# Four tiles in the first head's convolution, two of its three results stored from SyncE, and the first keys loaded over three queues

## The chip, the cores and the metric

The kernel runs on one core of a Trainium2 chip. The metric is the device time of one launch in microseconds (us). Engines are named as in the profile: PE is TensorE, DVE is VectorE, ACT is ScalarE, POOL is GpSimd, SP is SyncE. DMAs can be issued from SP, ACT and POOL; the profile calls their queues q1 (SP), q10 (ACT) and q0 (POOL).

## The reference

The input `x` has 48 channels of 256 x 256 pixels in float32. Two layers follow each other, each added to its input. Only the first touches the change:

```python
qkv = einsum('bchw,oc->bohw', group_norm(x), w_qkv)       # 48 -> 144 channels
qkv = depthwise_conv3x3(qkv, w_dw)
q, k, v = (heads(t) for t in split(qkv, 3))   # 4x4 patches, pad 4: 8 heads of 96 rows x 4356 patches
q, k = q / |q|, k / |k|
attn = softmax(einsum('bhcn,bhcm->bhnm', q, k) * temperature)
out = fold(einsum('bhcn,bhnm->bhcm', v, attn))
x = x + einsum('bchw,oc->bohw', out, w_proj)
```

The second layer normalises again and mixes 64 x 64 windows over width, height and channel. The 260 patches that lie wholly in the padding are zero, so the kernel works on the other 4096 only.

## The kernel before, in words

The program runs in stages. First it loads `x`, takes the group statistics, and writes the pointwise convolution of the first two heads to a tensor in DRAM (`t1`). Then `depthwise_first` (L358) does the depthwise convolution of head 0. Then the attention runs head by head, with the convolution of the next head woven into it by a hand-written order. The output projection and the second layer close the program.

`depthwise_first` works on ten "rows" (`Depthwise(0, r, dg)`). A row is 126 partitions (7 bands of the image x 18 channels: 6 each of q, k and v) of 4 x 256 pixels, and the bands lie 36 image lines apart. For each row the steps are:

- `load` (L209, issued from SP) brings 6 lines with margins into a tile `pad`.
- The nine taps are done either on VectorE (even rows: `first` on ACT, L215, then eight `tap`, L234) or as 18 matmuls with diagonal matrices on TensorE (odd rows, L223).
- `square` (ACT, L245), `reduce` (DVE, L249), `norm` (a matmul, L253) and `root` (L257 to L262) give the factor `y`.
- `scale` (DVE, L279) writes `o`, re-ordered to 16 x 64 per partition.
- `high` (ACT, L288) rounds `o` to `oh`; `low` (here on POOL, L292) writes the remainder `ol`.
- `store` (L297) issues three DMAs of 504 KB, of `oh`, `ol` and `o`, to the DRAM tensor `qkv[0]`. Each partition's 16 x 64 values go out as 16 pieces of 256 bytes, 2560 bytes apart.

The tiles come from the pool `dg`. The class takes their number from one line: `self.bufs` is 2 with a pool, and `pad` has twice as many (4). A tile can be written again when its last reader, a store included, is done. The order of the instructions on each engine in this stage is fixed when the program is built, by a scheduler that looks at the dependencies; the queues then run in that order.

After this stage every engine reads the value `large` and branches past a code path for large temperatures that isn't taken (L465). Then the attention's prologue loads the first query block (six DMAs on SP), the eight key tiles of head 0 and two value tiles:

```python
load_query(0, 0)
for m in range(NM):
    load_key(0, m, nc.scalar if m % 2 else nc.sync)
for m in range(2):
    load_value(0, m)
    turn(0, m)
```

`load_key(h, m)` issues four or eight DMAs (L313), eight where its 512 columns cross a border between two bands in `qkv`: four for tiles 0 and 7, eight for the others, 56 in all. They read what the stores wrote, so all wait for the landed stores. `scores` (L339) then multiplies queries and keys, `weigh` (L570) the exponentials and values.

Of the kernel before, what the change touches and what calls it, by code (L numbers as in the profile page):

```python
# [43 lines left out]
def conv_preact_kernel(  # L44
# [15 lines left out]
    nc = tc.nc  # L60
# [103 lines left out]
    def both_halves(t, y, n, base=0):  # L164

        return [t[:, base + s * HALF + y : base + s * HALF + y + n, :] for s in range(2)]

    class Strip:


        def __init__(self, j):
            self.j = j
# [20 lines left out]
        def store(self):  # L193
            for s, rows in enumerate(both_halves(t1[1], 2 * self.j, 2, base=1)):
                nc.sync.dma_start(out=rows, in_=self.ot[:, 2 * s : 2 * s + 2, :])

    class Depthwise:


        def __init__(self, h, r, pool=None):  # L200
            self.h, self.r = h, r
            self.pool, self.bufs = (pool, 2) if pool else (cv, 1)

        def load(self):
            g = [i for i, (h0, h1) in enumerate(GROUPS) if h0 <= self.h < h1][0]
# [85 lines left out]
            self.ol = self.pool.tile([NP1, KK, PX], F32R, name="ol", tag="t4", bufs=self.bufs)  # L291
            eng.tensor_sub(self.ol, self.o, self.oh.bitcast(F32))  # L292

        def store(self, parts=(0, 1, 2)):
            px = slice(self.r * PX, (self.r + 1) * PX)
            for i in parts:
                nc.gpsimd.dma_start(  # L297
                    out=qkv[self.h][i].rearrange("j (c k) n -> (j c) k n", k=KK)[:, :, px],
                    in_=self.o if i == 2 else (self.ol if i else self.oh).bitcast(F32),
                )  # L300
# [16 lines left out]
    def load_keys(kt, h, m, eng=nc.sync):  # L317
        col = m * 512, (m + 1) * 512
        k0, k1 = (qkv[h][i, :, HD : 2 * HD] for i in range(2))
        to = kt.bitcast(F32)  # L320
        load(to[0:HD, 0, :], k0, *col, eng)
        load(to[HD:128, 0, :], k1[:, 0:32], *col, eng)
        load(to[0:64, 1, :], k1[:, 32:], *col, eng)
        load(to[64:128, 1, :], k1[:, 32:], *col, eng)
# [35 lines left out]
    def depthwise_first():  # L360

        with tc.tile_pool(name="dg", bufs=1) as dg, tc.tile_pool(name="dps", bufs=3, space=PSUM) as dps:
            diag = dg.tile([NP1, 9, NP1], F32, name="diag")
            for t in range(9):
                nc.gpsimd.tensor_scalar_mul(diag[:, t, :], ident[:NP1, :NP1], dwt[:, 0, t : t + 1])
            rows = [Depthwise(0, r, dg) for r in range(CR + 1)]
            for d in rows[:2]:
                d.load()
            for i in range(0, CR + 1, 2):
                a, b = rows[i : i + 2]  # L370
                b.taps_on_tensor(diag, dps.tile([NP1, 2, 512], F32, name="dps"))
                a.first()
                for t in range(1, 9):
                    a.tap(t)
                for d in rows[i + 2 : i + 4]:
                    d.load()
                for d in (a, b):
                    d.square()
                    d.reduce()
                    d.norm()  # L380
                    d.root(on_scalar=True)
                    d.scale()
                    d.high()
                    d.low(nc.gpsimd)
                    d.store()


    with tc.tile_pool(name="xn", bufs=1) as xnp, tc.tile_pool(name="cst", bufs=1) as cst, tc.tile_pool(
# [10 lines left out]
        for j in range(0, HALF, LR):  # L399
            for s in range(2):  # L400
                eng = nc.sync if s == 0 else nc.scalar
# [10 lines left out]
        for g, (w, k) in enumerate(((wq, P2), (wr, C))):  # L412
            m = w.shape[1]
# [42 lines left out]
    cv = attention.enter_context(tc.tile_pool(name="cv", bufs=1))  # L456
# [3 lines left out]
    for t in ots:  # L460
        nc.gpsimd.memset(t[:, :, 0:1], 0.0)
        nc.gpsimd.memset(t[:, :, W + 1 : W + 2], 0.0)
    depthwise_first()

    with tc.If(nc.values_load(large) > 0):  # L465
# [33 lines left out]
    with tc.tile_pool(name="ahead", bufs=2) as ah, tc.tile_pool(name="ae", bufs=3) as ae, tc.tile_pool(  # L499
# [7 lines left out]
        def load_key(h, m, eng=nc.sync):  # L507
            keys[h, m] = ah.tile([128, 2, 512], F32R, name="kt", bufs=14)
            load_keys(keys[h, m], h, m, eng)
# [81 lines left out]

        load_query(0, 0)
        for m in range(NM):
            load_key(0, m, nc.scalar if m % 2 else nc.sync)
        for m in range(2):
            load_value(0, m)
            turn(0, m)
# [9 lines left out]
        with tc.manual_schedule():  # L607
            load_query(0, 1)
            block = scores(0, 0)
            for h in range(NH):  # L610
                more = h + 1 < NH
                rows = {r: Depthwise(h + 1, r) for r in range(CR + 1)} if more else {}
                for g in range(NG):
                    p, d, n = rows.get(g - 2), rows.get(g - 1), rows.get(g)
# [42 lines left out]
                    for k in range(NK):  # L657
# [25 lines left out]
                        if g == 0 and h > 0 and k == 0:  # L683
                            for m in range(6, 8):
                                store(h - 1, m)
                        if g == NG - 1 and k > 0:
                            for m in range(2 * k - 2, 2 * k):
                                store(h, m)
            for m in range(6, 8):
                store(NH - 1, m)  # L690
# [69 lines left out]
    with tc.tile_pool(name="lx", bufs=2) as lx, tc.tile_pool(name="lz", bufs=2) as lz, tc.tile_pool(  # L760
# [14 lines left out]
        xqs, rts, zts, blks, parts = {}, {}, {}, {}, {}  # L775
# [150 lines left out]
```

## Time and profile before

| | us |
|---|---|
| median of 3 runs (3830.28 to 3836.73) | 3835.93 |
| the profiled execution | 3845.87 |
| its span | 3844.1 |
| first store of `depthwise_first` issued | 188.0 |
| last one issued | 288.6 |
| first key load issued (ACT) | 301.4 |
| PE busy in the span | 3525.9 (92%) |
| DVE busy | 2199.1 (57%) |
| ACT busy | 1717.9 (45%) |
| POOL busy | 583.3 (15%) |

The 40 slices of the page show TensorE at nine tenths or more from the sixth slice (480 us) to the thirty-fourth; the first four slices hold the statistics, the pointwise convolution and `depthwise_first`. A share over the whole span says little on the change, which lies between 145 and 330 us: that stage is to be read by itself.

### The profile page before, as it was taken

The numbers are of one execution on the slowest core, as the hardware profiler recorded it, in microseconds if no ns is written. First come the engines' busy times: TensorE is split into PE (matmuls) and PEld (weight loads), VectorE is DVE, ScalarE is ACT, GpSimd is POOL, SyncE is SP. The second block draws the span as 40 slices with busy tenths as digits, with TensorE's granted clock in tenths as the row PEclk, the third lists the DMA queues.
The fourth block names the chain that finished last, engine by engine and source line by source line (L and its number), as shares of the span: only waits on it lengthen the run. The fifth ranks groups of instructions, "written<-read, shape, count | busy, mean of one in ns | idle before, by whom it ended". The sixth has DMA issues, their size and how long they took to land.

```text
span 3844.1 us, 99863 instructions
## 1 busy us (share of the span) xinstructions
PE 3525.9 (92%) x44216; PEld 2927.6 (76%) x44216; DVE 2199.1 (57%) x3520; ACT 1717.9 (45%) x2668; POOL 583.3 (15%) x535
## 2 busy tenths in 40 slices
PE   1856999999999999999999999999999999755998
PEld 0324777788888888888888888888888888514776
DVE  5562776169727962994399359826972222365553
ACT  0223565555545544554455455545554444200222
POOL 0150212012201220221022112201220000000111
PEclk9877999999999999999999999999999999866999
DMA  6475676534523443444244325433542000598555
GB/s 142 153 163 144 178 196 179 175 109 117 119 81 101 119 110 87 104 120 98 83 117 115 94 81 128 111 88 92 128 113 75 24 18 22 116 238 141 111 105 100
DMA packets 280235, 441.66 MB, mean 115 GB/s; under 512 B 57354, under 2 KB 205082, under 8 KB 276336
## 3 DMA queue, kind: packets, MB, share of 16 engines
q1 hardware_dynamic: 225150, 260.52, 26.7%
q0 software_dynamic: 48896, 165.90, 19.2%
q10 hardware_dynamic: 5746, 8.73, 1.0%
q8 instruction: 351, 5.75, 0.6%
q14 instruction: 92, 0.75, 0.1%
HBM read 234.76 MB, written 199.95 MB: 113 GB/s over the span
## 4 chain that ended last, share of the span: by engine, by line
PE 73%; issue 10%; DMA 8%; DVE 2%; SPq 1%; POOL 0%; ACT 0%; POOLq 0%; ACTq 0%; DVEq 0%
PE big L339 32%; PE big L570 31%; DMA lxq<-x1s 3%; PE pb L826 3%; PE pa L804 2%; PE big L183 2%; DMA pot<-os__70 2%; PE pc L843 1%; DMA qkv<-o 1%; DMA pxt<-in_x_dram 1%; PE pst L524 1%; PE pt L587 1%; PE pn L253 1%; DMA xs<-in_x_dram 1%; DMA kt<-qkv 1%
## 5 line engine op out<-in xcount | busy, mean ns | idle before, releaser
L541 ACT ACTIVATE e<-big,nmx 128x1024 f32<-128x1024 f32 x1024 | 1144.0, 1117 | 846.2 <-PE big L339 636.4
L339 PE MATMUL big<-kt,qt 128*128 128x512 f32 x6144 | 1441.9, 394 | 57.9 <-DMA kt<-qkv 54.9
L570 PEld LDWEIGHTS big<-vn,e 128*64 128x64 f32 x32768 | 1364.8, 137 | 87.7 <-ACT e L541 45.1
L570 PE MATMUL big<-vn,e 128*64 128x96 f32 x32768 | 1422.7, 248 | 9.1 <-ACT ot L186 4.0
L339 PEld LDWEIGHTS big<-kt,qt 128*128 128x128 f32 x6144 | 1147.9, 189 | 322.0 <-issue 63.1
L581 DVE TENSOR_TENSOR oacc<-big,oacc 128x768 f32<-128x768 f32 x480 | 458.2, 955 | 708.7 <-PE big L570 708.7
L234 DVE SCALAR_TENSOR_TENSOR acc<-pad,dwt,acc 126x1024 f32<-126x1024 f32 x600 | 779.3, 1300 | 34.2 <-ACT acc L215 18.5
L292 POOL TENSOR_TENSOR ol<-o,oh 126x1024 fp32r<-126x1024 f32 x80 | 189.9, 2373 | 909.1 <-DVE ss L249 810.1
L554 DVE TENSOR_REDUCE zt<-zs 128x1 f32<-128x4 f32 x256 | 38.8, 152 | 368.5 <-ACT e L541 368.5
L811 DVE TENSOR_TENSOR lzt<-pa,cbias 128x864 f32<-128x864 f32 (+1 forms) x88 | 136.3, 1621 | 134.5 <-PE pa L804 134.5
L541 ACT ACTIVATION_READ_ACCUMULATOR e<-big,nmx 128x1 f32 x1024 | 196.3, 192 | 0.0
L833 ACT COPY lyt<-pb 128x512 f32<-128x512 f32 x144 | 84.3, 586 | 250.0 <-PE pb L826 250.0
L297 POOL DMA_DIRECT2D qkv<-o x80 | 101.0, 1262 | 567.8 <-DVE zu L556 348.7
L245 ACT ACTIVATE sq<-acc 126x1024 f32<-126x1024 f32 x75 | 79.3, 1058 | 171.7 <-issue 111.6
L279 DVE TENSOR_TENSOR o<-acc,y 126x1024 f32<-126x1024 f32 x75 | 149.4, 1992 | 11.0 <-DMA qkv<-o 11.0
L826 PEld LDWEIGHTS pb<-wsb,lzt 128*64 128x64 f32 x2304 | 132.1, 143 | 28.1 <-issue 21.1
L715 PE MATMUL pps<-pot,wp 96*96 96x512 f32 x128 | 77.9, 778 | 77.6 <-DMA pot<-os__70 77.6
L826 PE MATMUL pb<-wsb,lzt 128*64 128x128 f32 x2304 | 147.9, 287 | 1.3 <-issue 1.3
L186 ACT ACTIVATE ot<-big,bias 108x1024 f32<-108x1024 f32 x64 | 71.0, 1112 | 147.8 <-PE big L183 68.2
L804 PE MATMUL pa<-csn,lxq 48*128 48x144 f32 x1024 | 95.1, 333 | 33.9 <-DMA lxq<-x1s 32.6
L590 POOL DMA_DIRECT2D os__70<-oo x64 | 32.6, 514 | 615.4 <-ACT oo L589 615.4
L715 PEld LDWEIGHTS pps<-pot,wp 96*96 96x96 f32 x128 | 26.9, 218 | 128.0 <-issue 126.4
(115 smaller groups left out, 1897.6 us busy)
## 6 DMA issues: line engine op xcount, KB each, us to landing
pad<-t SPq DMA_DIRECT2D x80, 761.9 KB
qkv<-o POOLq DMA_DIRECT2D x80, 504.0 KB, 6.9
qkv<-oh POOLq DMA_DIRECT2D x80, 504.0 KB, 7.4
qkv<-ol POOLq DMA_DIRECT2D x80, 504.0 KB, 9.1
t<-ot SPq DMA_DIRECT2D x128, 217.7 KB
qt<-qkv SPq DMA_DIRECT2D x176, 96.0 KB
xs<-in_x_dram SPq DMA_DIRECT2D x128, 96.0 KB
os__70<-oo POOLq DMA_DIRECT2D x64, 192.0 KB, 2.8
```

Of the source, the lines that this page charges most:

```text
L234: nc.vector.scalar_tensor_tensor(self.acc, self.pad[:, dy : dy + KS, dx : dx + W], dwt[:, self.h, tap : tap + 1], self.acc, ALU.mult, ALU.add,
L279: nc.vector.tensor_tensor(self.o.rearrange("p (a b) x -> p a b x", a=KS), self.acc.rearrange("p a (x b) -> p a b x", b=KS), self.y.rearran ...
L292: eng.tensor_sub(self.ol, self.o, self.oh.bitcast(F32))
L297: nc.gpsimd.dma_start(out=qkv[self.h][i].rearrange("j (c k) n -> (j c) k n", k=KK)[:, :, px], in_=self.o if i == 2 else (self.ol if i else ...
L339: nc.tensor.matmul(ps[:, i, :], lhsT=qt[:, r, q0 : q0 + 128], rhs=kts[2 * j + i][:, r // 2, :], start=(r == 0), stop=(r == 2),)
L541: nc.scalar.activation(e[:, j * 1024 : (j + 1) * 1024], ps.rearrange("p a b -> p (a b)"), AF.Exp, bias=nmx[:, b : b + 1], accum_out=zs[:, ...
L570: nc.tensor.matmul(ps[p : p + 64, j // 4, j % 4 * HD : (j % 4 + 1) * HD], lhsT=e[:, mb * 128 + p : mb * 128 + p + 64], rhs=vn, start=(i == 0),
L581: nc.vector.tensor_add(oaccs[h, k], ps[:, :, : 4 * HD], oaccs[h, k])
L715: nc.tensor.matmul(ps[:, i : i + 2, :], lhsT=wp, rhs=ot[:, ki * KS + i : ki * KS + i + 2, :], start=True, stop=True,)
L804: nc.tensor.matmul(pa[:, s, i * T3 * C : (i + 1) * T3 * C], lhsT=xq[r, y0 + i, :], rhs=csn[r], start=True, stop=True,)
L811: nc.vector.tensor_tensor(zv[:, :, y0 : y0 + n, :], pa[:, :, : n * T3 * C].rearrange("p s (y k) -> p s y k", y=n), cbias.rearrange("p (u v ...
L826: nc.tensor.matmul(pb[s * WS : (s + 1) * WS, i, :], lhsT=zts[u][:, t * C + c + i, :], rhs=wsb[:, t, :], start=True, stop=True,)
```

## The change

It has three parts. The convolution of head 0 gets four tiles of each kind instead of two (and eight `pad` instead of four). Its stores are issued one by one: `oh` from SP right after `high`, `ol` from POOL as before, `o` from SP. The first key tiles go round over ACT, SP and POOL (tiles 0, 3, 6; 1, 4, 7; 2, 5), 20, 20 and 16 DMAs.

```diff
-            self.pool, self.bufs = (pool, 2) if pool else (cv, 1)
+            self.pool, self.bufs = (pool, 4) if pool else (cv, 1)
...
-        def store(self, parts=(0, 1, 2)):
+        def store(self, parts=(0, 1, 2), eng=nc.gpsimd):
             px = slice(self.r * PX, (self.r + 1) * PX)
             for i in parts:
-                nc.gpsimd.dma_start(
+                eng.dma_start(
...
                     d.high()
+                    d.store((0,), nc.sync)
                     d.low(nc.gpsimd)
-                    d.store()
+                    d.store((1,))
+                    d.store((2,), nc.sync)
...
         for m in range(NM):
-            load_key(0, m, nc.scalar if m % 2 else nc.sync)
+            load_key(0, m, (nc.scalar, nc.sync, nc.gpsimd)[m % 3])
```

In the built program SP issues the ten `pad` loads first and then the twenty stores, in the order `o`, `oh`, `oh`, `o` for each pair of rows; POOL issues the ten `ol` stores, each after its subtraction. On VectorE the scalings of rows 3, 5 and 7 stand ahead of taps and reductions that they followed before. The other heads' convolutions take their tiles from another pool, and their stores and key loads are as they were.

## The prediction

> **What bounds the kernel now.** I read the chain that ended last first, then the stage table, then engine and DMA lines. From 332 us on the chain is TensorE at work (busy 455.7 of 468 us between 332 and 800), and the change leaves that loop alone. Before it lies a hole: the chain passes from store to store of `depthwise_first`, then from key load to key load.
>
> ```profile
> 251.14 9.91 DMA qkv<-o
> ...
> 268.06 13.49 DMA qkv<-o
> ...
> 288.60 12.52 DMA qkv<-o
> ...
> 327.72 2.05 PE big L339 x4
> ```
>
> Columns: start, length, what. The last store lands at 301.1, the last key feeds TensorE at 327.7. Whatever moves 327.7 moves the end by as much. First what holds the stores, on VectorE (start, length, instruction, idle before and its releaser), then per stage:
>
> ```profile
> 261.14 1.22 DVE L279 TENSOR_TENSOR o<-dps,y 126x1024 f32<-126x1024 f32 x1 [0.66 <-DMA qkv<-o]
> ...
> 274.42 1.97 DVE L279 TENSOR_TENSOR o<-acc,y 126x1024 f32<-126x1024 f32 x1 [11.05 <-DMA qkv<-o]
> 281.67 1.23 DVE L279 TENSOR_TENSOR o<-dps,y 126x1024 f32<-126x1024 f32 x1 [5.28 <-DMA qkv<-o]
> ```
>
> ```profile
> 255.00:301.00 46.00, 2.73 (x9) 1.30 (x7) 8.33 (x11) 7.30 (x9) 24.07 (x16) 0.55 0.77 155
> 188.00:255.00 67.00, 57.80 (x136) 25.43 (x135) 62.77 (x56) 16.58 (x21) 37.08 (x24) 0.92 0.70 172
> ```
>
> The last three scalings wait 17.0 us for an `o` tile whose store hasn't landed: two tiles are too few. Before 255 VectorE is busy 62.8 of 67 us, so it is the limit there. But the DMA share (last but one column) is 0.77 after 255: the stores are nearly a limit themselves. So I priced them by queue, 188 to 301 us:
>
> ```profile
> q0 software_dynamic: 4800, 15.52, 65.2%
> q1 hardware_dynamic: 519, 3.03, 7.3%
> ```
>
> 65.2% of 113 us x 16 engines is 1179 engine-us for 30 stores: 2.46 us of all 16 each. A store is 2016 runs of 256 B, 126 an engine: 19.5 ns a run, and a packet (160 per store) holds 12.6 runs.
>
> **What the Trainium skill says.** (1) "DMA: Bandwidth & Descriptors", the section on why a DMA increments its semaphore by 16: a DMA from SP or ACT uses the largest k up to 16 that divides the slowest dimensions of both sides. The pads (source outermost 7) agree, in the window 156 to 160:
>
> ```profile
> DMA packets 127, 0.74 MB, mean 186 GB/s; under 512 B 7, under 2 KB 7, under 8 KB 127
> ```
>
> Seven small closing packets per load, and a share of 0.444, about 7/16. For a store from SP, with 126 and 2016, k is 14; no run of before shows it. (2) Same page, "Queues, rings and completion order": queues take turns on an engine packet by packet; one ring is consumed in order. So stores on SP stand behind pads on SP. (3) Same page, "Why small descriptors are slow (HBM only)": each packet costs about 3 cycles beside 8 for 256 B. In the trace hardware packets hold one run, software packets 12.6, so the moved stores lose that sharing. (4) Same page, "Issuing engines are not separate DMA queues": spreading saves issue time only. Here issue is what the first keys lack (below).
>
> **The change, part by part.**
>
> *Four tiles.* Pads go from 4 to 8; `sq`, `ss`, `o`, `oh`, `ol` from 2 to 4; instruction counts stay. Removed: the 17.0 us of waits. VectorE's own work runs out at 263.4; without the waits the last `o` comes one dependent chain later, about 265 (y of row 9 near 263.4, scale 1.2), `oh` 1.04 later at 266, `ol` 2.33 later at 268, its issue 1.35. The scheduled order also takes `o` of rows 3, 5 and 7 ahead of taps, 5 to 10 us earlier. What is late next is the DMA. Pads: 4.2 us each on 7 engines (780 KB at 186 GB/s). Eight go out at once; rows 8 and 9 wait for the first two pads (free by 172), so these 7 engines carry pads until 150 + 10 x 4.2 + 3 = 195.
>
> *Stores from SP.* 20 of 30 leave GpSimd (20 issues of 1.23 to 1.48 us: 27 us off POOL, which is not on the path except for the last 2.7). On SP they are queued behind all ten pad issues, and nothing else of SP's waits there. Price of a 256 B run in a packet of its own, from loads, as before has no such store: low end
>
> ```profile
> q10 hardware_dynamic: 90, 0.02, 9.5%
> ```
>
> (302 to 303 us: 1.52 engine-us / 90 = 17 ns), and a mixed window, 2340 to 2345,
>
> ```profile
> q1 hardware_dynamic: 687, 0.27, 24.6%
> ```
>
> 19.7 engine-us / 687 = 28.6 ns at a mean of 393 B; at the pads' 186 / 7 = 26.6 GB/s an engine the 137 B in excess take 5 ns off. I take 24 ns, with ends 17 and 40 (twice the software run: a write may cost more than a read). A store is then 144 runs x 24 = 3.5 us of engines 0 to 13. A row costs these 2 x 3.5 + 2.46 (`ol`, still GpSimd) = 9.4 us. Ten rows from 195: 195 + 94 + 2 to land = 291, against 301.1: **-10 us**. Rows arrive in time for it (row 4 is scaled at 230, four rows are served by 233), so the DMA is the bound, no more VectorE. At 17 ns a row is 7.4, the arrivals decide, and it is about 281; at 40 ns it is 14, and 337.
>
> *SP arrives later at the branch.* Now SP is free at 222.8 and pays for the skipped branch under cover:
>
> ```profile
> L465 SPq EVENT_SEMAPHORE  x8: 17/17/17, 229.8 to 234.9; - x8
> L465 SPq TENSOR_LOAD <-large x1: 899/899/899, 222.8 to 222.8; - x1
> ```
>
> From the load of `large` to ready is 12 us. After the change it begins at SP's last store issue. In the later stage SP issues two loads of 1536 runs in 1.5 us and is then held, 3.7 us per load, so only some 200 runs an engine are taken in advance: SP is held until about 284, ready at 296, 5 us after the landing. **+5 us** on the queries; the keys on ACT and GpSimd don't wait for it. If the DMA is fast, this is hidden (266 + 12 = 278).
>
> *Keys on three queues.* 56 loads, 28 each on SP and ACT, at 0.74 and 0.82 us an issue:
>
> ```profile
> 301.41 22.85 ACTq L313 DMA_DIRECT2D kt<-qkv  x28
> ...
> 304.48 20.70 SPq L313 DMA_DIRECT2D kt<-qkv  x28
> ```
>
> SP and ACT share eight completion semaphores in the compiled program, each DMA waiting for the one eight before; GpSimd has eight of its own. Hardware issues fall from 62 (with six of queries) to 46: 16 fewer at 24 us / 62 = 0.39 is **-6 us**. GpSimd's 16 cost 0.52 each, 8 us, and land in 3.5 (from its later key loads); it has nothing else to do. From SP's start: queries 3, 20 keys at 0.55 = 11, landing 3, a last pair of logits 1: 18 us. So 296 + 18 = 314, against 327.7: -14; without SP's delay the DMA (4.6 MB at 200 to 250 GB/s, 20 us) gives 291 + 21, much the same.
>
> *Sum*: -10 + 5 - 6 is -11, and 20 SP issues at 0.55 instead of 0.74 with fewer ahead of them make the other 3: -14. The profiled execution is 3845.9 (span 3844.1) and becomes 3832; the median shown is 3835.9, so 3822. The loop after 332 starts earlier by this and its own waits (pads at 342.9, strips at 468) are relative to its start.
>
> **The rivals.**
>
> *The stores aren't a limit* (17 to 20 ns, landing near 281): for it the 17 ns window; against it that these were loads, 90 of them, beside little else. SP ready at 288, keys by 306: -22 us, 3814. Chance 0.25.
>
> *My sum* (21 to 27 ns): -8 to -20 us, 3822. Chance 0.37.
>
> *Gains cancel* (27 to 31 ns, or SP held longer): landing 298 to 308, change within 7.7 us, 3836. Chance 0.15.
>
> *Slower: hardware stores of 256 B runs become the bound.* At 40 ns a store is 5.8, a row 14, landing 337, keys 337 + 21 = 358: +30 us, 3866. It decides from 327.7 - 21.5 = 306, that is (306 - 197) / 10 = 10.9 a row, 4.2 a store, 29 ns a run. For it: 1536-run loads of 512 B in the last stage took 58 ns a packet (3500 to 3540 us: 117.6% of 640 engine-us / 12928); against it both windows above. Chance 0.23.
>
> That four tiles change nothing (the DMA alone set the pace) is part of the third: the last three rows would merely wait elsewhere.
>
> **How the numbers follow.** 0.2% is 7.7 us, about what a measurement of this kernel can tell from no change. Faster: the first two, 0.61 of 0.62. Same: 0.15, with 0.01 more. Slower: 0.23. The predicted time is the second case, 3822; its own range is 3816 to 3828. The range reaches down to the best case less a few us of keys, 3804, and up to 35 ns a run, landing 318 and +14, with a few us for SP, 3852.
>
> **What would show it.** Right: no VectorE wait for `qkv<-o`; last `o` near 265; queue q1 with about 2016 + 14 packets per moved store, 22 to 27 ns each; the last landing an SP store near 291; first key logits on ACT's loads, SP's queries up to 5 us after the landing; last key wait near 313. Wrong: q1 above 30 ns a packet, or a last landing past 306; then the stores should have stayed. If `ol` on GpSimd lands last, the ring and turn argument is wrong.

## The result and the profile after

The changed kernel takes 3819.33 us (median of 10 runs, 3815.44 to 3830.9) against 3835.18 us for the kernel before (10 runs, 3829.95 to 3844.42): 0.996 of the time, 95% interval 0.9947 to 0.9974, or about 16 us less. The profiled executions are 3816.70 (span 3814.9) and 3845.87 us. Their difference of 29 us is more than the medians differ by; 6 to 7 us of it arise in the last stages of the program, which the change doesn't touch. So the reading below stays in the stage between the first pad and the first logits.

VectorE's last scalings first (start, length, instruction; an idle time in brackets would follow). They answer to the 11.05 and 5.28 us of waits shown of before:

```profile
262.02 1.97 DVE L279 TENSOR_TENSOR o<-acc,y 126x1024 f32<-126x1024 f32 x1
264.89 1.23 DVE L279 TENSOR_TENSOR o<-dps,y 126x1024 f32<-126x1024 f32 x1
```

No wait for a store is left, and the last `o` is scaled at 264.89 instead of 281.67. Now SP's own timeline in the same form:

```profile
186.81 18.98 SPq L297 DMA_DIRECT2D qkv<-oh  x2
...
271.05 6.56 SPq L297 DMA_DIRECT2D qkv<-o  x1
286.05 3.02 SPq L313 DMA_DIRECT2D qt<-qkv  x6
289.12 16.89 SPq L313 DMA_DIRECT2D kt<-qkv  x20
```

SP's last store is issued at 277.6. Between there and the queries lies the skipped branch, by the trace's instructions of line 467 (the former 465):

```profile
L467 SPq EVENT_SEMAPHORE  x8: 17/17/17, 284.1 to 285.4; - x8
L467 SPq TENSOR_LOAD <-large x1: 1199/1199/1199, 277.7 to 277.7; - x1
```

The chain that ended last (start, length, what) goes from the queries and keys to the last wait of TensorE, which was at 327.72 before:

```profile
286.91 3.22 DMA qt<-qkv
...
305.24 3.15 DMA kt<-qkv
...
308.42 2.17 PE big L339 x7
```

Before and after don't begin this stage at the same moment: the first pad is issued at 149.52 before and at 147.82 after, and the stages ahead of it scatter by some us from run to run. From here on times are therefore counted from the first pad issue. **Ready** is the first key load on ACT (all stores landed, all engines past the branch), **stage** is the last wait of TensorE for a key, and **keys** is the difference. Each comes from one profiled execution.

| | last `o` scaled | ready | keys | stage |
|---|---|---|---|---|
| before | 132.2 | 151.9 | 26.3 | 178.2 |
| after | 117.1 | 137.7 | 22.9 | 160.6 |

The stage is 17.6 us shorter: 14.2 to ready, 3.4 with the keys.

### The profile page after: what moved, and what is told of

Its sections match the earlier page's. It is cut to its first block, busy times and chain, and to the rows that moved or that the text cites. A ratio compares the mean times of both kernels' runs of the same rounds, so it can differ in the third digit from the quotient of the medians.

```text
span 3814.9 us, 99860 instructions
## 1 busy us (share of the span) xinstructions
PE 3522.9 (92%) x44216; PEld 2924.4 (77%) x44216; DVE 2201.3 (58%) x3520; ACT 1717.0 (45%) x2668; POOL 566.6 (15%) x531
## 4 chain that ended last, share of the span: by engine, by line
PE 72%; issue 11%; DMA 8%; SPq 1%; DVE 1%; ACT 0%; POOL 0%; ACTq 0%; POOLq 0%
PE big L339 32%; PE big L572 31%; PE pb L828 3%; DMA lxq<-x1s 3%; PE pa L806 2%; DMA t<-ot 1%; PE big L183 1%; DMA pot<-os__70 1%; PE pc L845 1%; DMA pxt<-in_x_dram 1%; PE pst L526 1%; PE pt L589 1%; PE pn L253 1%; DMA x1s<-pxt 1%; SPq L313 0%
## 5 line engine op out<-in xcount | busy, mean ns | idle before, releaser
L297 POOL DMA_DIRECT2D qkv<-o x70 | 86.0, 1229 | 508.8 <-DVE zu L558 236.3
L828 PEld LDWEIGHTS pb<-wsb,lzt 128*64 128x64 f32 x2304 | 132.3, 143 | 28.6 <-issue 21.5
```

The lines of the kernel that those rows point to most:

```text
L297: eng.dma_start(out=qkv[self.h][i].rearrange("j (c k) n -> (j c) k n", k=KK)[:, :, px], in_=self.o if i == 2 else (self.ol if i else self. ...
L828: nc.tensor.matmul(pb[s * WS : (s + 1) * WS, i, :], lhsT=zts[u][:, t * C + c + i, :], rhs=wsb[:, t, :], start=True, stop=True,)
```

## The experiments

Three questions were put. Which of the three parts brought the gain: do the tiles and SP need each other, as the prediction's sum has it, or does one of them do it alone? Is the software queue what the stores lost their time to? And does SP, with its stores behind the pads, bound the new kernel? Each expectation says what its letters stand for in its own run. Two programs were profiled twice; their ready and stage differ by up to 1.5 us, so less than 2 us is not read.

### Each part alone

Only the four tiles (`e1_tiles`):

```diff
-            self.pool, self.bufs = (pool, 2) if pool else (cv, 1)
+            self.pool, self.bufs = (pool, 4) if pool else (cv, 1)
```

> Only the four tiles; all thirty stores on GpSimd, keys on two queues. Measure: from the first pad issue of the first head to the last key load that TensorE waits for (178.2 us before, 160.6 us with the whole change). Theory A (the waits for a free tile held the stage, and GpSimd's stores keep up): no VectorE wait for a store, last scaling about 117 us after the first pad, last GpSimd issue 10 us later, landing 12 us after it, keys 26 us: about 165, that is -13 us in the stage and in the time. Rival B (the DMA rate held it, tiles only move the waits): about 176, -2 us or less.

Only `oh` and `o` on SP, with two tiles and the keys on two queues (`e2_sp`):

```diff
                     d.high()
+                    d.store((0,), nc.sync)
                     d.low(nc.gpsimd)
-                    d.store()
+                    d.store((1,))
+                    d.store((2,), nc.sync)
```

> Only the move of two stores to SP; two tiles, keys on two queues. Theory A: the waits for a free tile stay, and a tile now waits for stores that share 14 engines in ring order, so VectorE's waits grow from 17 us; the stage is 178 to 186 us long, time 0 to +8 us. Rival B (the gain of the whole change is the faster issue from SP): 165 to 170, -8 to -13 us.

Only the keys (`e3_keys`):

```diff
-            load_key(0, m, nc.scalar if m % 2 else nc.sync)
+            load_key(0, m, (nc.scalar, nc.sync, nc.gpsimd)[m % 3])
```

> Only the first keys over three queues. Theory A (the eight completion semaphores that SP and ACT share set the pace of the key loads): last store landed to last key falls from 26.6 to about 21 us, time -5 us. Rival B (the keys move at the rate of the DMA engines, or are held by SP's queries): 25 to 26.6 us, time -1 us or none.

Tiles and SP, with the keys as before (`e4_nokeys`, the changed kernel with the last line taken back):

> The whole change without its last part: four tiles, two stores on SP, keys on two queues. Theory A: 3 to 5 us longer than the whole change in the stage (164 to 166), time -12 us against before. Rival B (the third queue does nothing, since SP comes late to the branch and its queries decide): 161, time as with the whole change, -16 us.

| | last `o` scaled | ready | keys | stage | time, ratio to before (95%) |
|---|---|---|---|---|---|
| `e1_tiles` | 120.7 | 148.6 | 25.3 | 173.9 | 0.9986 (0.9975 to 0.9997) |
| `e2_sp` | 121.0 | 139.1 | 26.9 | 166.0 | 0.9954 (0.9935 to 0.9972) |
| `e3_keys` | 132.3 | 152.7 | 24.1 | 176.8 | 0.9982 (0.9973 to 0.9992) |
| `e4_nokeys` | 118.8 | 139.8 | 26.1 | 165.9 | 0.9952 (0.9934 to 0.9969) |

The move of two stores to SP is worth 12.2 us in the stage by itself. The four tiles are worth 4.3 alone and nothing on top of SP (165.9 against 166.0), though two tiles had been named as what holds VectorE. How that can be is in the profiles. With the tiles alone VectorE's last scalings come without a wait:

```profile
264.01 1.97 DVE L279 TENSOR_TENSOR o<-acc,y 126x1024 f32<-126x1024 f32 x1
266.87 1.23 DVE L279 TENSOR_TENSOR o<-dps,y 126x1024 f32<-126x1024 f32 x1
```

Against before they are 11.4 us earlier (counted from the first pad), but the stores don't land earlier by as much. Two windows of `e1_tiles` (start to end, length, then PE, PEld, DVE, ACT, POOL busy and in brackets the instructions, the TensorE clock, the share of the 16 DMA engines, GB/s), POOL's last store, and ACT's first key:

```profile
255.00:280.00 25.00, 6.23 (x17) 2.94 (x15) 6.95 (x10) 5.80 (x8) 20.01 (x14) 0.65 0.93 177
280.00:295.00 15.00, 0.00 (x0) 0.00 (x0) 0.00 (x0) 0.00 (x0) 0.00 (x0) 0.50 0.59 124
```

```profile
277.36 1.88 POOL L297 DMA_DIRECT2D qkv<-o  x1
```

```profile
294.72 22.10 ACTq L313 DMA_DIRECT2D kt<-qkv  x28
```

The software queue runs at a share of 0.93 and is still 15 us behind when POOL has issued its last store, so it isn't POOL's issuing that holds the stores. The share is 0.59 over these 15 us; the DMA view doesn't tell the engines apart, so whether some of them had run dry is not shown. From the last scaling to ready it takes 27.9 us, 8 more than the 19.7 of before. So the waits of VectorE were a sign of late landings, and the additional tiles only moved the queue from in front of VectorE to behind it.

With SP and only two tiles the landings are early enough for two tiles nearly to do. One wait of 3.27 us is left, and the stage is none the longer for it:

```profile
269.68 1.23 DVE L279 TENSOR_TENSOR o<-dps,y 126x1024 f32<-126x1024 f32 x1 [3.27 <-DMA qkv<-o]
```

The keys give 2.2 us alone and 3.2 on top of the rest; counted to the start of the next four logit matmuls, which depends less on how the last loads fall, it is 3.4 both times. In time, `e2_sp`, `e4_nokeys` and the whole change can't be told apart: their ratios are 0.9954, 0.9952 and 0.9960, and the intervals overlap. What the keys add to SP is seen in the stage alone.

### How many stores on SP

All three results on SP (`e6_allsp`, the changed kernel with this edit), and once more in the same series as the changed kernel itself (`e10_allsp`, `e11_after`); only `oh` on SP (`e7_onesp`):

```diff
-                    d.store((1,))
+                    d.store((1,), nc.sync)
```

> The whole change with the third result too stored from SP; GpSimd only subtracts. Theory A (a hardware store costs 2.8 us of 14 engines, and what gained was two queues sharing the load, with the software stores on all 16): a row costs 3 x 2.8 = 8.4 us instead of 8.0, the last landing is 3 to 6 us later and SP is held longer: stage 164 to 168. Rival B (hardware queues are better in themselves; the tail of the software queue, 5 to 8 us with few engines at work, was the loss): 158 to 160.

```diff
-                    d.store((2,), nc.sync)
+                    d.store((2,))
```

> The whole change with only the rounded result on SP; the remainder and the unrounded one on GpSimd, one behind the other. Theory A (balance between the queues, a row is 2.8 + 2 x 2.46 = 7.7 us on the busiest engines): the same as the whole change, 160 to 162. Rival B (every software store that remains adds its share of the software queue's loss; 11 us for twenty moved): about 166.

> The kernel with all three results on SP, four tiles and three key queues once more, beside the whole change on one chip: theory A (each software store moved is worth about 0.3 us) 3 to 4 us faster than the whole change in stage and time; rival (the first comparison was chance): within 2 us of it.

> The whole change again, as the partner of the kernel with all stores on SP: -16 us against before, stage 160 to 161 us.

| stores on POOL | | last `o` scaled | ready | time, ratio to before (95%) |
|---|---|---|---|---|
| 30 | `e1_tiles` | 120.7 | 148.6 | 0.9986 (0.9975 to 0.9997) |
| 20 | `e7_onesp` | 120.8 | 143.4 | 0.998 (0.9967 to 0.9993) |
| 10 | after | 117.1 | 137.7 | 0.996 (0.9947 to 0.9974) |
| 10 | `e11_after` | 116.6 | 139.2 | 0.9963 (0.9943 to 0.9983) |
| 0 | `e6_allsp` | 116.4 | 135.3 | 0.9937 (0.992 to 0.9954) |
| 0 | `e10_allsp` | 116.5 | 135.3 | 0.9954 (0.9934 to 0.9975) |

All have four tiles; `e1_tiles` has its keys on two queues, the others on three, which comes after ready. Every ten stores taken off the software queue make ready some 2 to 6 us earlier.

Part of this comes through VectorE: its last scaling is 4.3 us earlier without stores on POOL than with thirty, though in none of these runs does VectorE wait for a store. The forty taps of `e1_tiles`, and of `e6_allsp` below (busy us and mean ns of one after the bar):

```profile
L234 DVE SCALAR_TENSOR_TENSOR acc<-pad,dwt,acc 126x1024 f32<-126x1024 f32 x40 | 62.2, 1573 | 17.9 <-ACT acc L215 17.0
L234 DVE SCALAR_TENSOR_TENSOR acc<-pad,dwt,acc 126x1024 f32<-126x1024 f32 x40 | 57.7, 1460 | 18.0 <-ACT acc L215 17.1
```

Those of `e1_tiles` take 4.5 us longer, and four taps hold all of it. The longest lasts 4.83 us in `e1_tiles`, 3.97 in after and 3.37 in `e6_allsp`, where the median is 1.28. In these three runs every tap above 1.4 us coincides with a subtraction of POOL, in the first two with its store issues as well. That POOL's work stretches them is read from this coincidence; no run tests it by itself. The rest of the gain lies behind the last scaling: from there to ready it takes 27.9 us with thirty stores on POOL, 22.6 with twenty, 20.6 and 22.6 with ten, 18.9 with none.

In `e6_allsp` hardware stores are alone on the DMA engines for a while, and show their price. The DMA view of its window 205 to 225 (total; then queue, kind, packets, MB, share of 16 engines), and below it the stage window that answers to the first one of `e1_tiles`:

```profile
DMA packets 16186, 4.11 MB, mean 206 GB/s; under 512 B 16186, under 2 KB 16186, under 8 KB 16186
...
q1 hardware_dynamic: 16186, 4.11, 94.5%
```

```profile
255.00:280.00 25.00, 2.97 (x9) 1.44 (x8) 6.32 (x9) 5.21 (x7) 4.64 (x2) 0.59 0.91 198
```

94.5% of 20 us x 16 engines is 302 engine-us for 16186 packets: 18.7 ns is the mean length of a packet's record. It is tempting to read from the 94.5% that more than 14 engines work, but the records overlap, and the share can pass 100%. A window of `e8_padpool`, 160 to 180 us:

```profile
q0 software_dynamic: 1190, 3.41, 102.5%
```

What tells the engines is the number of closing packets, by which the prediction read seven engines for the pads. Between 226 and 247 us of `e6_allsp`, with the queue empty at both ends, six stores are moved:

```profile
q1 hardware_dynamic: 12180, 3.10, 67.6%
```

12180 is 6 x (2016 + 14); with 16 closing packets a store it would be 12192. So a store from SP runs on **14 engines**, as predicted. At 16186 packets in 20 us one of them takes 14 x 20 / 16186 = **17.3 ns a packet of one run**, and a store of 2030 packets 2.5 us. SP issues at about that pace while it is held:

```profile
272.12 2.47 SPq L297 DMA_DIRECT2D qkv<-ol  x1
274.69 2.33 SPq L297 DMA_DIRECT2D qkv<-o  x1
```

In the same stretch, 255 to 280, DMA moved 177 GB/s in `e1_tiles`, nearly all of it from the software queue, and 198 in `e6_allsp` (with a hole of 1.5 us in it). What the software queue has besides is its tail of 15 us behind the last issue: POOL isn't held and runs ahead of its stores. In `e6_allsp` SP is held, its last issue ends at 277.0, and the keys start at 282.45.

`e10_allsp` and `e11_after` took 3819.2 and 3823.66 us side by side. Their intervals overlap, so the time doesn't tell them apart; the stage does, with the same step twice: 156.0 against 159.5, and 157.0 against 160.6 in the first pair. The query block's next four matmuls after the last key wait start at 161.1 against 164.9 from the first pad, 3.8 earlier, and in the first pair (`e6_allsp`, after) at 159.0 against 162.9, 3.9 earlier. The version with all three on SP has the shortest stage seen.

### Is SP what holds it now?

Four pads instead of eight, at four tiles of the rest (`e5_pad4`), since the second SP store of after was held for 16.6 us behind ten pads:

```diff
-            self.pad = self.pool.tile([NP1, KS + 2, W + 2], F32, name="pad", bufs=2 * self.bufs)
+            self.pad = self.pool.tile([NP1, KS + 2, W + 2], F32, name="pad", bufs=4 if self.bufs == 4 else 2)
```

> The whole change with four pad tiles instead of eight (the other tiles stay at four). With eight, SP was held 16.6 us on one store while the DMA share fell to 0.1 to 0.2: its first stores stood in the ring behind pads on seven engines. Theory A (those stores are early, the last landing is decided 80 us later): the hold goes, the stage from first pad issue to last key stays at 160 +-2 us, time as with the whole change. Rival B (the hole is work lost and delays every later store): 155 us, 5 us faster than the whole change.

That hold is gone: the first two `oh` stores take 10.2 us together, as seven pads now stand ahead of the stores and three between them. The stage is 161.6 against 160.6, the time 0.9952 (0.9937 to 0.9967): no difference. A hold of SP while later work has time is free.

The pads from POOL instead of SP, with the setting up of `diag` moved from POOL to VectorE (`e8_padpool`; the cut shows one of the two places of the load):

```diff
-                d.load()
+                d.load(nc.gpsimd)
```

> A try for more: the whole change with the first head's pads loaded from GpSimd and the diagonal matrices made on VectorE, which has nothing to do at that point. From GpSimd the pads should use all 16 engines (1.9 us each) instead of 7 (4.2 us). Theory A (VectorE's and TensorE's start is late by the first pads): first taps 2 to 4 us sooner, TensorE's first matmul 4 to 5 us sooner, last scaling and stage 3 to 5 us shorter: 156. Rival B (the stage is set by the stores alone): last scaling sooner, stage unchanged at 160; Rival C: GpSimd's descriptor writing meets VectorE's taps and the start is later.

A miss. Instead of freeing the stores, it delayed the pads. ACT's first reading of a pad, with the pads issued at 149.35:

```profile
159.18 1.15 ACT L215 ACTIVATE acc<-pad,dwt 126x1024 f32<-126x1024 f32 x1 [17.06 <-DMA pad<-t]
```

That is 9.8 us after the issue, against 7.6 in after (147.82 to 155.39); its second reading comes at 20.9 against 15.7. VectorE has `diag` done by 150.5, so that isn't the reason. The last scaling comes at 122.1 instead of 117.1, ready at 141.7 instead of 137.7, and the group of seven logit matmuls that has the last key wait of after starts at 164.4 instead of 160.6. The time is 0.9967 (0.9953 to 0.9982).

All three stores on SP without the four tiles and without the keys (`e9_spalone`, the kernel before with one edit):

```diff
-                    d.store()
+                    d.store(eng=nc.sync)
```

> The kernel before with all thirty stores on SP and nothing else: two tiles, keys on two queues. Theory A (the software queue was the loss, and with hardware stores of 2.4 us the second tile is free in time): stage from first pad to last key 161 to 164 us against 178.2, no wait for a tile above 3 us, time -14 to -17 us, nearly all of what the whole change gains. Rival B (with everything in one ring the two tiles, and pads queued on SP behind stores, bind again): 168 to 172, -6 to -10 us.

It keeps next to nothing, less than either theory had: 0.9995 (0.998 to 1.0009), ready 147.8, stage 174.0. SP's timeline shows why:

```profile
240.72 2.37 SPq L297 DMA_DIRECT2D qkv<-o  x1
243.14 2.89 SPq L209 DMA_DIRECT2D pad<-t  x2
```

With four `pad` tiles the loads of the last rows are issued between stores, and each store ahead of them holds SP for 2.4 us. The pads come late, and the last scaling is at 130.0 (280.37), 14 us later than with all on SP and eight pads. VectorE was busy for 50.1 of the 67 us from 188 to 255, against 63.1 in `e6_allsp`; one wait of 5.4 us for a store's tile is among its waits too. So the four tiles, worth nothing beside two stores on SP, are what makes three stores on SP pay: with eight pads all loads are issued ahead of the first store. (`e9_spalone` also lacks the third key queue, which comes after ready, and has `oh` stored after the subtraction in the program's order.) Whether the pads or the other tiles of the four do it was not tried separately; most of what the timeline shows late is pads.

## Why the prediction was right, and where it wasn't

The forecast was 3822 us and the result 3819.33; 14 us of gain were expected at the last key wait and 17.6 came in the stage. The sum was nearly right, in part by luck: the stores were faster than forecast and the keys gained less, and the two errors lie in opposite directions.

- **The bound was read rightly, its cause not.** The stage before the attention holds the 16 us that the medians show. But "two tiles are too few" took the releaser of a wait for its cause. The waits went as foreseen (last `o` forecast near 265, seen at 264.89, or 266.6 on the clock of before, where the first pad is 1.7 later), and `e1_tiles` shows that this alone lets the stores land only 3.3 us earlier. `e2_sp` shows the other half: with early landings, two tiles cost 3.3 us of wait and no stage time. The prediction had the pieces for this: it said that the stores were nearly a DMA limit and that the DMA is late next. It didn't ask what each part was worth without the other.
- **The price of a hardware store was the mis-sized term.** The 14 engines were right; they had been worked out from the Trainium skill, "DMA: Bandwidth & Descriptors", the section on why a DMA increments its semaphore by 16, and the closing packets of the stores agree, as those of the pads did. But the 24 ns a run became 17.3, and 3.5 us a store 2.5. The records of after are about as long as those of `e6_allsp`, 19.3 ns against 18.7 (200 to 220 us: 60.8% of 320 engine-us over 10062 packets):

```profile
q1 hardware_dynamic: 10062, 2.61, 60.8%
q0 software_dynamic: 208, 0.69, 16.3%
```

  The same page's "Why small descriptors are slow (HBM only)" was the ground for expecting a loss where a packet holds one run: the software runs had cost 19.5 ns in packets of 12.6 runs, so no loss showed. A row is 2 x 2.5 + 2.46 = 7.5 us instead of 9.4. That is the 17 ns end of the prediction, "the arrivals decide, and it is about 281"; SP's last packets ran until about 283.6, or 285.3 on the clock of before, where 291 had been forecast. So the first rival had the mechanism of the stores, and not the forecast case.
- **SP at the branch**: forecast 5 us after the landing, on the queries alone; seen about 2, and on all queues. The forecast took the 12 us of before, from the load of `large` to ready, for a price. After, SP was held until 277.6 and ready for the queries at 286.05, 8.4 us, and most of that is waiting (total, times, longest):

```profile
SPq L467 <- SPq L467: 6.0, 2, 5.1
```

  The wait of 5.1 ends at 284.1, just behind SP's last packets. That it is for its own stores is read from this order of times. Before, the same row gives 10.6 us of the 12, so that was no fixed price either. "The keys on ACT and GpSimd don't wait for it" failed: ACT's keys begin at 285.54, POOL's at 286.08, and POOL had waited 12.9 us for SP's instructions of the branch:

```profile
286.08 8.19 POOL L313 DMA_DIRECT2D kt<-qkv  x16 [12.92 <-SPq L467]
```

- **The keys**: forecast 6 us and 3 more through SP; measured 2.2 to 3.4. POOL's 16 took the 8 us foreseen, but 20 on SP took 16.89 us, 0.84 each, where 0.55 had been assumed. SP and ACT still issue most of them, and the chain after still ends in SP's issues and their keys.
- **The slower rival** needed 29 ns a run; nothing near it was seen. The 58 ns of the last stage's loads, quoted for it, were no guide to these stores: they come from a share of 117.6%, so the records overlapped and their length is not an engine's time.
- **Two sums are slightly off**: by the prediction's own formula 31 and 35 ns a run land at 311 and 322, not 308 and 318. Neither case came.

In the sum: ready was taken as 10 earlier for the landing less 5 for SP, and came 14.2 earlier with SP's 2 in it; the keys as 9, and came as 3.4.

## What to carry to other kernels

A wait for a tile doesn't say that tiles are too few: ask whether the transfer that frees it would land in time if there were more of them, and if the DMA queue is behind, move or speed the queue first. When a kernel issues many small-run stores from POOL late in a stage, price the tail behind the last issue, not only the share of the DMA engines. Read the number of engines from the closing packets, not from the share: records overlap. On an engine that issues in order, put all loads that later work needs ahead of stores that hold it; the spare tiles that allow this may be worth nothing until then.

## What the hardware showed that wasn't expected

- Hardware stores of 256-byte runs, one run to a packet, took 17.3 ns of an engine each on 14 engines and moved 206 GB/s over 20 us, 2.5 us a store. The software queue, with 12.6 runs to a packet and work waiting all the time, moved 177 GB/s in 25 us of `e1_tiles`, 2.9 us a store. Sharing packets bought nothing here.
- The software queue had 15 us of work left behind POOL's last issue in `e1_tiles`.
- A VectorE tap of 1.28 us lasted up to 4.83 us where it coincided with POOL's subtraction and store issues, and up to 3.37 with the subtraction alone. With the stores off POOL the last scaling came from 120.7 us after the first pad to 116.4.
